# q, k and the attention scores laid out over four row groups, with a new order of the steps

## The chip, the cores and the metric

The kernel runs on one core of one Trainium2 chip. The metric is the device time of one execution in microseconds (us), from the first to the last instruction of the core; a profiled execution also gives the span and, for every engine, the instructions with their start and duration. The engines are called TensorE (PE in the profile, PEld for its weight loads), VectorE (DVE), ScalarE (ACT), GpSimd (POOL) and SyncE (SP, which issues the transfers). They run side by side[...], and semaphores tie them together.

## What is computed

Two layers of a "metaformer" over 32 images of 56 x 56 positions with 96 channels. Layer 0 is window attention (windows of 7 x 7 = 49 positions, three heads of 32 channels) and a feed-forward block, layer 1 a scan along the image's width (a linear recurrence, computed here as a product with a Toeplitz matrix) and a second feed-forward block. Cut to what the change touches:

```python
qkv = xs @ w_qkv + b_qkv                                   # 96 -> 3 x 96
q, k, v = (to_windows(t) for t in split(qkv))              # [image, head, window, 49, 32]
att = einsum('bhwid,bhwjd->bhwij', q, k) * scale + pos_bias
att = att.at[:, :, -nw_w:].add(ul_mask)
out = einsum('bhwij,bhwjd->bhwid', softmax(att), v)
x = x + (out @ w_out + b_out)
x = x + ffn0(norm(x));  x = x + scan(norm(x));  x = x + ffn1(norm(x))
```

## The kernel before

The work is cut into blocks: a quarter of an image, two rows of windows, 16 windows, 784 positions; 128 blocks in all. Everything that is done to a block is a *step* with a short name (`step[...]`, defined with `@steps`): `LD` loads it, `sa`, `pa`, `na`, `ta`, `ea` normalise and transpose it, `q`, `k`, `v` multiply by the weights on TensorE, `eq`, `ek`, `ev` copy the results out of PSUM on ScalarE, `sc` makes the scores, `st0` to `st2` scale them and add the bias on VectorE (one head each), `ex0` to `ex2` take the exponential on ScalarE, `av` multiplies by v, `rc` divides, `tro`, `eo`, `pr`, `ad` project and add. The feed-forward blocks are `s p n t e h x r c y z b k` with the letter `f` or `g`; `h` is a product on TensorE, `x` its copy to 16 bits on ScalarE, `r` bias and maximum on VectorE, `c` the cast to 8 bits (number 1 of three on GpSimd), `y` the second product, `k` the addition to the block on GpSimd. The scan has `se` to `xe`, `r0`, `pu0` to `pu3`, `th`, `uc`; six units `SC0` to `SC5` with `GA0` to `GA5` once per image, that is in every fourth block; then `gt`, `eg`, `so`, `as`. `ST` stores the block.

The order is written out by hand in a table (`PIPELINED`, line 55): a list of entries `name:lag`. The loop in `pipeline` (line 864) runs 140 iterations; iteration t issues, in the order of the table, every step for block t minus its lag. An extra dependency keeps each engine to exactly this order, so the table is the order of every queue. An iteration thus holds one step of each kind, of up to twelve different blocks; four iterations make an image, and one or two of the four hold the six scan units as well.

PSUM has four buffers of two banks (`banks`, line 117). Every step on TensorE takes one (`sc` two) and the reader's last instruction frees it; a step that finds none free waits. A second table, `IN_TURN`, and the steps `any` and `av_any` are for inputs outside a bound and do not run here.

`q` and `k` (line 515) are each two products: stationary 96 columns of the weights, moving 392 positions. A product in 32 bits appears in the trace as two weight loads and two matmuls, so each step has 4. The results lie in `qT` and `kT`, channels on partitions 0 to 95, a head on 32 of them, all 784 positions along the row. `scores` (line 554) takes each of 16 windows and 3 heads: stationary 64 keys of 32 channels, moving 49 queries. The three heads sit on three of the four groups of 32 rows of the array, even and odd windows on its two halves of 64 columns. The results of heads 0 and 1 fill the two banks of one buffer, those of head 2 one bank of a second.

Of the kernel before, what the change touches and what calls it, by code (L numbers as in the profile page):

```python
# [8 lines left out]
F32 = mybir.dt.float32  # L9
# [4 lines left out]
ALU = mybir.AluOpType  # L14
# [9 lines left out]
C = 96  # L24
# [3 lines left out]
NH = 3  # L28
HD = 32
# [8 lines left out]
NBLK = 4  # L38
NRP = NBLK * G
NTOK = G * TP  # L40
NPAIR = 8
W2 = WS * WS
OVER = 64 - W2
HALF = NPAIR * W2
MASKED = -1.0e30
LNC_EPS = 1e-6
LNT_EPS = 1e-5
SSM_EPS = 1e-3
QSCALE = float(C) ** -0.5
# [3 lines left out]


PIPELINED = (
    "pu0:4 SC5:8 bg:10 xf0:3 pu2:4 xf2:3 pu3:4 pg:9 ng:9 th0:4 sa:1 uc0:4 GA5:8 ex2:2 ex0:2 th2:4 "
    "rf2:3 hf1:3 rf0:3 pu1:4 uc2:4 tg:9 th3:4 uc3:4 xf1:3 uc1:4 av:2 pa:1 gt1:8 cf2:3 cf0:3 rf1:3 "
    "kg:10 rc:2 th1:4 SC3:7 eg:9 hg1:9 eg1:8 cf1:3 na:1 yf:3 xg1:9 zf:3 GA3:7 tro:2 bf:3 eo:2 hg2:9 "
    "kf:3 xg2:9 rg1:9 rg2:9 SC1:7 gt0:8 GA1:7 cg2:9 ST:11 hg0:9 eg0:8 pr:2 xg0:9 LD:0 ad:2 ta:1 ea:1 "
    "sf:2 se:3 SC4:7 pf:2 so:8 GA4:7 as:8 q:1 pe:3 nf:2 eq:1 v:1 cg1:9 ne:3 ev:1 SC2:7 rg0:9 k:1 "  # L60
    "cg0:9 ek:1 tf:2 sg:8 ef:2 SC0:7 GA2:7 GA0:7 te:3 sc:1 xe:3 st1:1 r0:3 st2:1 st0:1 yg:9 ex1:1 "
    "zg:9 hf0:2 hf2:2 "
)

IN_TURN = (
# [10 lines left out]
def kernel(  # L76
# [27 lines left out]
    nc = tc.nc  # L104
# [12 lines left out]
    def banks(name):  # L117

        return psum.tile([128, 2, 512], F32, tag="ps", name=name)
# [112 lines left out]
    n = 1  # L232
# [166 lines left out]
        vs.append(v)  # L399
    ot = const.tile([128, G, 2 * NPAIR, WS], F32, name="ot")  # L400
    nc.vector.memset(ot[C:], 1.0)
    qT = const.tile([C, NTOK + OVER], F32, name="qT")
    nc.vector.memset(qT[:, NTOK:], 0.0)
    kT = const.tile([C, NTOK + OVER], F32, name="kT")
    nc.vector.memset(kT[:, NTOK:], 0.0)
    pT = const.tile([128, NH, HALF + OVER], F32, name="pT")
    nc.vector.memset(pT[:, :, HALF:], 1.0)
    xs = const.tile([128, G, 3, RS], F32, name="xs")
# [84 lines left out]
    @steps("LD")  # L493
    def _(i):
        xb = xpool.tile([TP, G, C], F32, tag="xb", name=f"xb_{i}")
        for dst, src in block_dmas(i, x, xb):
            nc.sync.dma_start(dst, src)
        xtiles[i] = xb
# [15 lines left out]

    @steps("q", "k")
    def _(i, n):
        pq = banks(f"qk_{i}_{n}")
        for half in range(2):
            nc.tensor.matmul(  # L519
                pq[0:C, half, 0:HALF],  # L520
                wqkv[:, n * C : (n + 1) * C],
                xws[i % 2][:, half * HALF : (half + 1) * HALF],
                start=True,
                stop=True,
            )
        held["qk", i, n] = pq

    @steps("eq", "ek")
    def _(i, n):
        dst = (qT, kT)[n][:, 0:NTOK].rearrange("c (h t) -> c h t", h=2)  # L530
        nc.scalar.copy(dst, held.pop(("qk", i, n))[0:C, :, 0:HALF])  # L531

    @steps("v")
    def _(i):
# [17 lines left out]
        )  # L552

    def scores(i, stat, mov):
        pab, pc = banks(f"sab_{i}"), banks(f"sc_{i}")
        dst = [pab[:, 0], pab[:, 1], pc[:, 0]]
        for w in range(2 * NPAIR):
            p0, n0 = (w % 2) * 64, (w // 2) * W2
            for h in range(NH):
                hp = slice(h * HD, (h + 1) * HD)  # L560
                nc.tensor.matmul(
                    dst[h][p0 : p0 + 64, n0 : n0 + W2],
                    stat[hp, w * W2 : w * W2 + 64],
                    mov[hp, w * W2 : (w + 1) * W2],
                    start=True,
                    stop=True,
                )
        return [d[:, 0:HALF] for d in dst]

    def scaled(dst, i, ps):  # L570
        bt = bias[i % NBLK == NBLK - 1].rearrange("p w q -> p (w q)")
        nc.vector.scalar_tensor_tensor(dst, ps, QSCALE, bt, op0=ALU.mult, op1=ALU.add)  # L572


    @steps("sc")
    def _(i):
        held["s", i] = scores(i, kT, qT)

    @steps("st0", "st1", "st2")
    def _(i, h):  # L580
        scaled(pT[:, h, 0:HALF], i, held["s", i][h])

    @steps("ex0", "ex1", "ex2")
    def _(i, h):
# [2 lines left out]
    @steps("any")  # L587
    def _(i):

        for h, ps in enumerate(scores(i, qT, kT)):  # L590
            pr = one.tile([128, 8 * C], F32, tag="an", name=f"pr_{i}_{h}")
            nc.vector.memset(pr[:, HALF : HALF + OVER], 0.0)
            pa = pr[:, 0:HALF]
            p3 = pa.rearrange("p (w k) -> p w k", k=W2)
            scaled(pa, i, ps)
            mx = two.tile([128, NPAIR], F32, tag="mx", name=f"mx_{i}_{h}")
            nc.vector.tensor_reduce(mx, p3, op=ALU.max, axis=AX.X)
            nc.vector.tensor_tensor(p3, p3, mx[:, :, None].to_broadcast([128, NPAIR, W2]), ALU.subtract)
            nc.scalar.activation(pa, pa, AF.Exp)

            pp = banks(f"pp_{i}_{h}")
            for w in range(2 * NPAIR):
                p0, n0 = (w % 2) * 64, (w // 2) * W2
                nc.tensor.matmul(
                    pp[p0 : p0 + 64, 0, n0 : n0 + W2], pr[:, n0 : n0 + 64], ident[:, p0 : p0 + W2], start=True, stop=True
                )
            nc.scalar.copy(pT[:, h, 0:HALF], pp[:, 0, 0:HALF])
# [334 lines left out]
```

## Time and profile before

| What | Value |
|---|---|
| Median of 7 runs (lowest to highest) | 3890.18 us (3889.07 to 3901.09) |
| The profiled execution: its own time, and its span | 3903.86 us, 3902.1 us |
| ACT, POOL: share of the span | 61%, 37% |
| Row of `eq`: ACT L531, 96 x 784, mean | 808 ns |
| Row of `ek`: ACT L531, 96 x 784, mean | 811 ns |
| Row of `eo`: ACT L660, 96 x 392, mean | 515 ns |
| Row of `st0` to `st2`: DVE L572, 128 x 392, mean | 557 to 559 ns |

A share of busy time is an average over the whole span. A matmul's duration contains time in which the next one already runs, so for TensorE it is of more use to take the time from a step's start to the start of the next, which the timeline of the engine gives.

### The profile page before, as it was taken

The page shows a single profiled execution, that of the slowest core. Times are in us where ns is not written, and L with a number is a line of the kernel's source. Part 1 is how long each engine was busy: PE and PEld are TensorE (multiplying, and loading weights), DVE is VectorE, ACT ScalarE, POOL GpSimd, SP SyncE. Part 2 cuts the span into 40 slices and gives each one's busy share as a digit, 9 for nine tenths or more (in the row PEclk, how much of TensorE's full clock was granted, in tenths as well). Part 3 has the DMA queues.
Part 4 walks back from the last instruction along what each step waited for, and adds up shares of the span by engine and source line. Part 5 has one row for each costly group of instructions (what it writes and reads, how often), then busy time and mean ns, then how long its engine had stood idle before and what let it go on. Part 6 is the DMA issues. An engine that isn't in the chain of part 4 may idle for free.

```text
span 3902.1 us, 174541 instructions
## 1 busy us (share of the span) xinstructions
PE 3716.9 (95%) x76580; PEld 3174.4 (81%) x76580; DVE 3207.5 (82%) x9292; ACT 2392.9 (61%) x4611; POOL 1456.7 (37%) x1176
## 2 busy tenths in 40 slices
PE   2799999999999999999999999999999999999996
PEld 1688888888888888888888888888888888888874
DVE  3668888888888888888888888888888888888864
ACT  0656666666666666666666666666656666666652
POOL 1223334433334333334433333433333443333332
PEclk7989999999999999999999999999999999999996
DMA  6000111001101011001010010100100101001000
GB/s 129 17 3 22 25 24 26 23 22 25 25 22 28 21 24 25 22 22 28 23 26 21 22 28 21 28 21 22 27 23 22 27 21 28 21 22 28 18 15 21
DMA packets 226255, 99.12 MB, mean 25 GB/s; under 512 B 218396, under 2 KB 225150, under 8 KB 225262
## 3 DMA queue, kind: packets, MB, share of 16 engines
q1 hardware_dynamic: 222522, 86.81, 9.8%
q8 instruction: 606, 9.93, 1.0%
q10 hardware_dynamic: 2964, 1.05, 0.1%
q14 instruction: 163, 1.34, 0.1%
HBM read 44.45 MB, written 43.35 MB: 23 GB/s over the span
## 4 chain that ended last, share of the span: by engine, by line
PE 76%; DVE 17%; issue 2%; ACT 2%; DMA 2%; SPq 0%; POOL 0%; DVEq 0%; ACTq 0%; POOLq 0%
PE pu L778 12%; PE scan L802 10%; PE qk L519 6%; PE so L856 6%; PE av L622 5%; PE gt L835 5%; PE pu L779 4%; PE py_f L724 4%; PE ph_f L690 3%; PE pv L538 3%; PE tr_o L651 3%; DVE xn_f L457 3%; PE pr L670 3%; PE py_g L724 3%; PE ph_g L690 3%
## 5 line engine op out<-in xcount | busy, mean ns | idle before, releaser
L778 PE MATMUL pu<-weg,xs 128*128 128x288 f32 x1792 | 614.8, 425 | 9.2 <-ACT h_f L702 7.1
L802 PE MATMUL scan<-u,toep 64*64 64x28 f32 x24576 | 411.8, 221 | 19.5 <-issue 19.3
L802 PEld LDWEIGHTS scan<-u,toep 64*64 64x64 f32 x24576 | 386.7, 136 | 52.9 <-issue 42.9
L447 POOL TENSOR_TENSOR rs_a<-rs_a,neg_half 112x7 f32<-112x7 f32 x128 | 231.5, 1808 | 524.5 <-DVE rs_a L441 524.5
L779 PEld LDWEIGHTS pu<-weg,xs 128*128 128x128 f32 x1792 | 341.3, 190 | 95.5 <-issue 0.5
L519 PE MATMUL qk<-xw,wqkv 128*96 128x392 f32 x1024 | 393.7, 507 | 7.3 <-ACT xw L513 7.3
L746 POOL TENSOR_TENSOR xb<-xb,y_f 112x672 f32<-112x672 f32 x128 | 201.2, 1572 | 534.0 <-DVE y_f L742 398.2
L531 ACT COPY qT<-qk 96x784 f32<-96x784 f32 x128 | 103.5, 808 | 465.5 <-PE qk L519 465.5
L856 PE MATMUL so<-wso,gT 128*112 128x96 f32 x3584 | 374.9, 262 | 3.4 <-ACT gT L845 3.4
L856 PEld LDWEIGHTS so<-wso,gT 128*112 128x112 f32 x3584 | 362.3, 178 | 7.6 <-ACT gT L845 5.7
L447 POOL TENSOR_TENSOR rs_f<-rs_f,neg_half 112x7 f32<-112x7 f32 x128 | 190.6, 1489 | 462.9 <-DVE rs_f L441 462.9
L702 ACT CAST h_g<-ph_g 128x784 f16<-128x784 f32 x384 | 314.6, 821 | 69.2 <-PE ph_g L690 69.2
L767 POOL COPY xs<-xs 96x392 f32<-96x392 f32 x128 | 65.3, 510 | 759.7 <-issue 755.9
L845 ACT COPY gT<-gt 96x672 f32<-96x672 f32 (+1 forms) x256 | 209.3, 818 | 195.1 <-PE gt L835 195.1
L778 PEld LDWEIGHTS pu<-weg,xs 128*128 128x128 f32 x1792 | 280.4, 192 | 58.4 <-DVE pT L572 38.1
L779 PE MATMUL pu<-weg,xs 128*128 128x96 f32 x1792 | 321.2, 261 | 0.0
L702 ACT CAST h_f<-ph_f 128x784 f16<-128x784 f32 x384 | 307.0, 840 | 0.4 <-PE ph_f L690 0.2
L708 DVE TENSOR_SCALAR h_f<-h_f,b1q 128x784 f16<-128x784 f16 x384 | 276.0, 747 | 34.3 <-ACT h_f L702 33.8
L708 DVE TENSOR_SCALAR h_g<-h_g,b1q 128x784 f16<-128x784 f16 x384 | 208.4, 543 | 108.2 <-ACT h_g L702 108.2
L817 DVE SCALAR_TENSOR_TENSOR gt<-gt,scan 128x448 f32<-128x448 f32 x384 | 220.2, 615 | 78.8 <-PE scan L802 78.6
L457 DVE TENSOR_SCALAR xn_f<-xb,st_f,rs_f 112x96 fp8e5<-112x96 f32 x896 | 278.3, 385 | 3.0 <-POOL rs_f L447 3.0
L791 ACT COPY u<-pu 128x384 f32<-128x384 f32 (+1 forms) x512 | 228.3, 446 | 81.0 <-PE scan L802 45.5
(151 smaller groups left out, 9176.9 us busy)
## 6 DMA issues: line engine op xcount, KB each, us to landing
xb<-in_x_dram SPq DMA_DIRECT2D x224, 126.0 KB
out_dram<-xb SPq DMA_DIRECT2D x224, 126.0 KB
taps_d<-u SPq DMA_DIRECT2D x1, 4704.0 KB
xb<-in_x_dram SPq DMA_DIRECT2D x224, 13.1 KB
xb<-in_x_dram SPq DMA_DIRECT2D x224, 7.9 KB
out_dram<-xb SPq DMA_DIRECT2D x224, 13.1 KB
out_dram<-xb SPq DMA_DIRECT2D x224, 7.9 KB
xb<-in_x_dram SPq DMA_DIRECT2D x32, 72.0 KB
```

The source lines that it names most:

```text
L447: nc.gpsimd.tensor_tensor(rs, rs, neg_half, ALU.pow)
L457: nc.vector.tensor_scalar(xn[:, g, :], xb[:, g, :], mean[:, col], rs[:, col], op0=ALU.subtract, op1=ALU.mult, **saturate)
L519: nc.tensor.matmul(pq[0:C, half, 0:HALF], wqkv[:, n * C : (n + 1) * C], xws[i % 2][:, half * HALF : (half + 1) * HALF], start=True, stop=True,
L690: nc.tensor.matmul(ph[:, half, 0:HALF], w1q[:, hc * 128 : (hc + 1) * 128], xqs[layer][:, half * HALF : (half + 1) * HALF], start=True, sto ...
L702: nc.scalar.copy(h16.rearrange("p (h t) -> p h t", h=2), held.pop(("ph", n, i, hc))[:, :, 0:HALF])
L708: nc.vector.tensor_scalar(h16, h16, b1q[:, hc : hc + 1], 0.0, op0=ALU.add, op1=ALU.max)
L724: nc.tensor.matmul(po[:, g - g0, :], hq[hc][:, g * TP : (g + 1) * TP], w2q[:, hc, :], start=(hc == 0), stop=(hc == 2),)
L778: nc.tensor.matmul(pu[:, g, 0 : E + EH], rows[:, 0:128], weg[:, 0 : E + EH], start=True, stop=True)
L779: nc.tensor.matmul(pu[:, g, E + EH : 2 * E], rows[:, RS:], weg[:, E + EH :], start=True, stop=True)
L791: nc.scalar.copy(u[:, rp : rp + n, :], held["pu", i, j][:, 0:n, E : 2 * E])
L802: nc.tensor.matmul(py[o0 : o0 + RS, eh, e * NRP : (e + 1) * NRP], toep[p * RS : (p + 1) * RS, ch * HW : ch * HW + RS], u[p * RS : (p + 1) ...
L856: nc.tensor.matmul(po[:, g - g0, :], gT[:, g - g0, eh, :], wso[:, eh, :], start=(eh == 0), stop=(eh == 1))
```

## The change

It has two parts.

First, the layout. `qT` and `kT` give way to two arrays. `qk01` holds q and k of heads 0 and 1: its 128 partitions are four groups of 32, group g being head g mod 2 of the block's half g // 2 (eight windows). `qk2` holds q and k of head 2: group g is windows 4g to 4g + 3. The step named `q` now makes all of `qk01`, in four products (64 columns of weights, 392 positions), of which those of the two halves go to different halves of the array's columns. The step named `k` makes all of `qk2`, in eight products (32 columns of weights, 196 positions), the four quarters on the four column groups. `ek` copies 128 x 392 where it copied 96 x 784. `scores` has the same 48 products as before, but on all four row groups, each with a bank of its own in the same two buffers. Heads 0 and 1 are now each spread over both banks of one buffer, and head 2 over both buffers, so `st2` becomes two VectorE instructions of 128 x 196 and `st0`, `st1` read two runs of 196.

Second, the table `PIPELINED`. It has the same 117 steps in another order, most with a lag one higher; the store's lag is 11 as before, the load's 0. The scan units stood one behind `pu0`, then five in the next part of one iteration (`SC5:8`, and `SC3 SC1 SC4 SC2 SC0` with lag 7); now they are `SC1 SC3 SC4 SC2` in one iteration (lag 8) and `SC0 SC5` at the start of the next (lag 9).

```diff
 PIPELINED = (
-    "pu0:4 SC5:8 bg:10 xf0:3 pu2:4 xf2:3 pu3:4 pg:9 ng:9 th0:4 sa:1 uc0:4 GA5:8 ex2:2 ex0:2 th2:4 "
-    "rf2:3 hf1:3 rf0:3 pu1:4 uc2:4 tg:9 th3:4 uc3:4 xf1:3 uc1:4 av:2 pa:1 gt1:8 cf2:3 cf0:3 rf1:3 "
-    "kg:10 rc:2 th1:4 SC3:7 eg:9 hg1:9 eg1:8 cf1:3 na:1 yf:3 xg1:9 zf:3 GA3:7 tro:2 bf:3 eo:2 hg2:9 "
-    "kf:3 xg2:9 rg1:9 rg2:9 SC1:7 gt0:8 GA1:7 cg2:9 ST:11 hg0:9 eg0:8 pr:2 xg0:9 LD:0 ad:2 ta:1 ea:1 "
-    "sf:2 se:3 SC4:7 pf:2 so:8 GA4:7 as:8 q:1 pe:3 nf:2 eq:1 v:1 cg1:9 ne:3 ev:1 SC2:7 rg0:9 k:1 "
-    "cg0:9 ek:1 tf:2 sg:8 ef:2 SC0:7 GA2:7 GA0:7 te:3 sc:1 xe:3 st1:1 r0:3 st2:1 st0:1 yg:9 ex1:1 "
-    "zg:9 hf0:2 hf2:2 "
+    "rf2:4 r0:5 hf0:4 GA2:9 cf1:4 SC0:9 zg:11 GA0:9 ex2:3 ex0:3 pu1:5 SC5:9 xf0:4 pu0:5 th1:5 av:3 "
+    "cf2:4 GA5:9 bg:11 uc1:5 pu2:5 th0:5 sa:1 rc:3 ta:2 rf0:4 uc0:5 uc2:5 th2:5 cf0:4 pa:1 ea:2 pg:10 "
+    "tro:3 yf:4 eo:3 kg:11 gt0:9 zf:4 pr:3 ng:10 pu3:5 bf:4 eg0:9 kf:4 ad:3 th3:5 sf:3 uc3:5 pf:3 k:2 "
+    "tg:10 se:4 ek:2 pe:4 SC1:8 gt1:9 eg:10 eg1:9 q:2 GA1:8 eq:2 hg0:10 nf:3 xg0:10 hg1:10 rg0:10 "
+    "SC3:8 xg1:10 ne:4 so:9 SC4:8 as:9 hg2:10 GA3:8 ST:11 v:2 tf:3 cg0:10 GA4:8 xg2:10 sc:2 ev:2 te:4 "
+    "ef:3 rg1:10 hf1:3 xe:4 rg2:10 cg2:10 cg1:10 st1:2 st2:2 xf1:3 ex1:2 hf2:3 xf2:3 SC2:8 st0:2 "
+    "yg:10 sg:9 na:1 LD:0 rf1:3 "
 )
...
     @steps("q", "k")
     def _(i, n):
+        parts, h0, h1 = ((2, 0, 2), (4, 2, 3))[n]
+        size, rows = NTOK // parts, 128 // parts
         pq = banks(f"qk_{i}_{n}")
...
+        for m in range(2):
+            for j in range(parts):
+                nc.tensor.matmul(
+                    pq[j * rows : (j + 1) * rows, m, 0:size],
+                    wqkv[:, m * C + h0 * HD : m * C + h1 * HD],
+                    xws[i % 2][:, j * size : (j + 1) * size],
+                    start=True,
+                    stop=True,
+                )
+        held["qk", i, n] = pq[:, :, 0:size]
...
     @steps("eq", "ek")
     def _(i, n):
+        dst = (qk01[:, :, 0:HALF], qk2[:, :, 0:QUARTER])[n]
+        nc.scalar.copy(dst, held.pop(("qk", i, n)))
...
     def scores(i, stat, mov):
+        tiles = [banks(f"s{n}_{i}") for n in range(2)]
+
+        def product(src, size, g, w, col):
+            gp = slice(g * HD, (g + 1) * HD)
+            p0, n0 = (w % 2) * 64, col + w // 2 * W2
+            nc.tensor.matmul(
+                tiles[g % 2][p0 : p0 + 64, g // 2, n0 : n0 + W2],
+                src[gp, stat, w * W2 : w * W2 + 64],
+                src[gp, mov, w * W2 : (w + 1) * W2],
+                start=True,
+                stop=True,
+            )
+
+        for w in range(NPAIR):
+            for g in range(4):
+                product(qk01, HALF, g, w, 0)
+            if w % 2:
+                for w2 in (w // 2 * 2 % 4, w // 2 * 2 % 4 + 1):
+                    for g in range(2 * (w // 4), 2 * (w // 4) + 2):
+                        product(qk2, QUARTER, g, w2, QUARTER)
+        return tiles
```

## The prediction

> **What bounds the kernel now.** I read the page, then the groups by shape, the timeline of TensorE over one iteration, the stretches of one iteration and one image, and last the instruction queue in the DMA view.
>
> ```profile
> PE 3716.9 (95%) x76580; PEld 3174.4 (81%) x76580; DVE 3207.5 (82%) x9292; ACT 2392.9 (61%) x4611; POOL 1456.7 (37%) x1176
> ...
> PE 76%; DVE 17%; issue 2%; ACT 2%; DMA 2%; SPq 0%; POOL 0%; DVEq 0%; ACTq 0%; POOLq 0%
> ```
>
> TensorE is busy 95% and carries 76% of the chain of waits; VectorE carries most of the rest. Groups by shape:
>
> ```profile
> L802 PE MATMUL scan<-u,toep 64*64 64x28 f32 x24576 | 411.8, 221 | 19.5 <-issue 19.3
> L519 PE MATMUL qk<-xw,wqkv 128*96 128x392 f32 x1024 | 393.7, 507 | 7.3 <-ACT xw L513 7.3
> L538 PE MATMUL pv<-wqkv,xw 128*64 128x96 f32 x4096 | 199.7, 251 | 0.0
> L561 PE MATMUL sc<-qT,kT 32*64 32x49 f32 x4096 | 167.3, 224 | 3.5 <-issue 3.5
> ```
>
> The mean durations overlap, so I take starts from TensorE's timeline:
>
> ```profile
> 2023.55 1.48 PE L519 MATMUL qk<-xw,wqkv 128*96 128x392 f32 x4
> 2024.97 1.54 PE L538 MATMUL pv<-wqkv,xw 128*64 128x96 f32 x32
> 2026.44 1.56 PE L519 MATMUL qk<-xw,wqkv 128*96 128x392 f32 x4
> 2027.83 0.51 PE L470 MATMUL tr_f<-ident,xn_f 112*96 112x112 fp8e5 x7
> ```
>
> Start to start, q takes 1.42 us, v 1.47, k 1.39. Stretches (columns: length, then busy time of PE, PEld, DVE, ACT, POOL, granted clock, DMA):
>
> ```profile
> 2038.06:2063.40 25.34, 25.34 (x409) 21.54 (x407) 23.50 (x70) 18.45 (x37) 11.10 (x10) 1.00 0.11 26
> 2063.40:2104.46 41.06, 39.60 (x1176) 34.90 (x1174) 29.55 (x82) 19.00 (x37) 13.04 (x10) 0.96 0.08 19
> 2400.00:2515.40 115.40, 114.49 (x2395) 98.08 (x2394) 99.57 (x290) 74.46 (x145) 45.34 (x36) 1.00 0.10 24
> ```
>
> A plain iteration takes 25.34 us, an image 115.40. With every step of TensorE at the shortest interval it shows, a plain iteration is 25.0 and a scan unit 2.00, so an image would be 4 x 25.0 + 6 x 2.00 = 112.0. The other 3.4 us are waits: some 1.2 behind the scores (hf2 and pu0 wait for buffers that st2 and st0 free, 0.35 per iteration) and 2.2 around the scan units, the interesting ones:
>
> ```profile
> 2065.72 1.95 PE L802 MATMUL scan<-u,toep 64*64 64x28 f32 x118
> 2068.73 0.36 PE L802 MATMUL scan<-u,toep 64*64 64x28 f32 x10 [1.06 <-issue]
> 2069.02 0.61 PE L690 MATMUL ph_g<-xq,w1q 128*128 128x392 fp8e5 x2
> 2069.42 2.15 PE L724 MATMUL py_f<-w2q,hq_f 128*112 128x96 fp8e5 x21
> ```
>
> TensorE stands still with nothing to wait for: its instructions haven't arrived. Its instruction queue brings 606 packets, 9.93 MB, for 153160 instructions: about 256 each. In the busiest parts packets follow each other at no less than about 3.3 us, so some 76 instructions per us is the supply; a scan unit uses 256 in 2.00 us. The table sets where that bites: SC3 right behind av, sc right behind SC0.
>
> **What the Trainium skill says.** "TensorE: Matmul & The Clock Gate", Part 3, says small products in different row or column groups run at once. The trace agrees: pv, on two column halves, starts its matmuls in pairs 82 ns apart, so 32 take 1.47 us rather than 2.6. "TensorEngine Tiling (Array Packing)", Tiling Modes, says that changing the tiling mode drains the engine. The trace shows a price: tr_e before the scores takes 0.76 us where tr_a, the same shape before a full product, takes 0.67; tr_g before av 0.44, tr_f 0.35; pv's end adds about 0.09 again. "TensorE: Matmul & The Clock Gate", Part 1, halves the clock after idling; after the stop above the clock was 0.50 from 2070 to 2072. "SBUF — State Buffer", Who interferes with whom, says that GpSimd and VectorE's fast modes lock one pair of ports against each other. Timelines of VectorE, then GpSimd:
>
> ```profile
> 2037.62 1.70 DVE L708 TENSOR_SCALAR h_f<-h_f,b1q 128x784 f16<-128x784 f16 x1
> ```
> ```profile
> 2037.64 1.46 POOL L746 TENSOR_TENSOR xb<-xb,y_g 112x672 f32<-112x672 f32 x1
> ```
>
> That step takes 0.42 us elsewhere in the same iteration.
>
> **The change, part by part.**
>
> *q and k.* A pass over 392 positions takes 0.33 us (1.32 for four), and each product is two passes. New q: 4 products, 8 passes on two column halves, 4 x 0.33 = 1.32, no less than before. New k: 16 passes of 196 positions on four groups, 4 x 0.166 = 0.66. Ends cost as v's: 1.47 - 16 x 0.082 = 0.15 each, and entering the mode 0.09. Before, q stood next to v and v next to k, so three steps shared two changes; the new order is gt1 q hg0, pu3 k tg, hg2 v tf, so each pays its own: q 1.32 + 0.24 = 1.56, k 0.66 + 0.24 = 0.90, v 1.56, sum 4.02 against 4.27. Gain 0.25 per block. Bounds: four column groups are not shown. If only two run at once k is 1.57 and the step loses 0.4; if the mode changes cost nothing it gains 0.65.
>
> *Scores.* Now 96 passes lie on six tiles of the array, 16 each, from first to last start 1.04 us: 65 ns per pass; SC needs 58 on four tiles. On eight tiles 12 passes x 0.062 + 0.15 = 0.89; but head 2 loads groups 0 and 1 in the first half and 2 and 3 in the second, and if the queue can't reach across it is 16 x 0.062 + 0.15 = 1.14. I take 1.02 against 1.19: 0.17 per block, bounds 0.05 and 0.3.
>
> *The other engines.* st2 becomes two instructions; from the rows of L489 (384 elements 553 ns, 288 448) half of 392 saves 0.21 of the 0.475 us from start to start, so two take 0.52: 0.05 more on VectorE. ek falls from 811 to about 515 ns (row of eo, same length); ScalarE, 18.45 busy in 25.34, gains nothing on the path.
>
> *Supply.* k and q have 32 more instructions per block (+4%). What counts is the instructions in a stretch against 76 per us, plus the 64 that the engine's queue holds by the first table of the page on TensorE (no run here shows that number). Before: SC2, k, tf, SC0, te, sc have 740 in 7.8 us (593 supplied, 80 short); av, gt1, SC3 have 460 in 4.3 us (327, 70 short). New, the worst runs from SC4 through v, sc, SC2, SC0, SC5 to av: 1590 in 19.2 us (1460, 66 short); no single unit stands next to av or sc without 0.7 us of long products between. One shortage in place of two, and it comes after SC1 and SC3 with room around them: of the 2.2 us I leave 0.9 + 0.2 for mode changes. Gain 1.1 per image; bounds 2.0 and -0.8 (several stops, each with a half clock).
>
> *Transfers.* SP holds only ST and LD. ST waits for kg, LD for ST; kg moves up to lag 11, so a load comes about one iteration nearer to its use. The load then lies between kg (about 10 us into an iteration) and sa of the next one, some 20 us, against about 5 us for a store and a load seen in the DMA view. No cost.
>
> *Waits of the new order.* After sc come te, hf1, hf2, yg. te and hf1 take 1.09 us; st1 and st2 need 1.0 and a handover, st0 0.5 more: hf2 and yg together wait about 0.35, as before. ScalarE's chain ev, ef, xe, xf1, ex1, xf2 ends 1.6 us into the next iteration, before pu0 needs xf2's buffer, and ex0 ends just as av wants it (3.2 us). So I charge the same 1.2 per image.
>
> *Both ends.* In both tables the second load stands behind the large Toeplitz transfer (sa waits 41.1 us for it once), and from sa at lag 1 to ST at lag 11 there are as many iterations. Nothing.
>
> Sum: 128 x (0.25 + 0.17) = 54, 32 x 1.1 = 35, together 89 us. Profiled execution 3903.86 - 89 = 3815, times 3890.18 / 3903.86 (the profiled run lies 0.35% above the median): **3802 us**.
>
> **Rivals.**
>
> *The array gives nothing* (four column groups in pairs, or mode changes eat it): only the supply's 35, less some for k: about 3856. For it: nothing before shows four groups; against: pv's pairs.
>
> *The order also removes VectorE's waits*, and the supply stops fully: 54 + 38 + 64 = 156, 3735. For it: 3.4 us per image are there to take. Against: VectorE is busy 23.5 of 25.34.
>
> *Slower: VectorE's loop decides.* Place: from the end of pr, VectorE must do ad 0.85, sf 1.2, wait for pf on GpSimd 0.35 beyond se 1.2, nf 2.25, rg0 0.42, ne 1.7, as 0.85, cg0 0.5, rg1, rg2 0.84, cg2 0.5, st1, st2 1.0: 11.7; then TensorE from hf2 through yg to the end of the next pr: 12.5; handovers 0.2. The loop is 24.4 us, with TensorE's own 24.9 just above. rf2 now comes with cf1 on GpSimd, rg2 with cg1, each able to block it 0.8 us or more. With one on the loop it is 25.2, as before; with two 26.0. Beyond 1.0 us of blocking the change loses: with 1.9 in every iteration, an image is 4 x 26.3 + 12.0 + 0.9 = 118.1, +2.7: 3976. In half the iterations it is about no change.
>
> **How the numbers follow.** Forecast 0.50 (its own range 3765 to 3845), array gives nothing 0.16, waits gone too 0.09, slower 0.25, of which 0.05 ends near no change; 0.03 of the second does as well. Below 0.2% nothing can be told apart here (the runs before mostly lie within that). So faster 0.72, same 0.08, slower 0.20. The range takes in both ends of the bounds, 3735, and on the other side the milder half of the loop's cases: 3915.
>
> **What would show it.** Right: k from start to start near 0.8 us plus a mode change, q still 1.4 to 1.5, scores near 1.0; plain iterations of 24.6 to 25.1; TensorE's waits for "issue" in the scan below 30 us in all. Wrong: k at 1.4 or more; stops of 1 us with the clock at 0.5 in many images; hf2, yg or yf waiting for VectorE by more than 0.7 us per iteration, with a 16-bit step of 1.2 us or more ahead of it.

## The result, and the profile after

The changed kernel takes 3879.58 us (median of 15 runs, 3874.93 to 3888.66), beside 3891.55 us for the kernel before on the same chip (35 runs). The ratio is 0.9969, with a 95% interval of 0.9963 to 0.9976. So it is faster by 0.3%, which is outside the noise, and by 12 us where 88 us were forecast; 3802 us lies far off, and the range (3735 to 3915) holds the time. The profiled execution took 3876.86 us, its span is 3875.1 (before: 3902.1). The profiled execution of the kernel before was a long one, 12 us above the median of its kernel, so the two pages lie 27 us apart where the kernels lie 12 apart.

Two lines of the page of the changed kernel, the busy time of the engines and the shares of the chain of waits:

```profile
PE 3699.8 (95%) x78628; PEld 3126.1 (81%) x78628; DVE 3244.9 (84%) x9420; ACT 2330.7 (60%) x4611; POOL 1453.5 (38%) x1176
...
PE 90%; DVE 6%; DMA 2%; issue 1%; ACT 0%; POOL 0%; SPq 0%; ACTq 0%; DVEq 0%; POOLq 0%
```

TensorE's share of the chain went from 76% to 90%, VectorE's from 17% to 6%. By itself that says little: the page of the new layout with the old table, a slower kernel, has 88% and 3%. TensorE is still busy 95%, so "busy" says nothing of the change either. Its groups by shape:

```profile
L830 PE MATMUL scan<-u,toep 64*64 64x28 f32 x24576 | 408.3, 221 | 15.3 <-issue 14.2 <-ACT u L819 0.5
L526 PE MATMUL qk<-xw,wqkv 128*64 128x392 f32 x1024 | 198.6, 509 | 0.3 <-issue 0.3
L545 PE MATMUL pv<-wqkv,xw 128*64 128x96 f32 x4096 | 197.6, 249 | 0.0
L568 PE MATMUL s<-qk 32*64 32x49 f32 x12288 | 172.0, 228 | 1.7 <-issue 1.7
L526 PE MATMUL qk<-xw,wqkv 128*32 128x196 f32 x2048 | 112.8, 338 | 2.3 <-ACT xw L516 2.3
```

q and k together are busy 311 us where they were 394, the scores 172 where they were 170 (both groups of line 561 together). TensorE's timeline in one plain iteration (start, duration; the distance to the next start is what counts), k first and then the scores with what follows them:

```profile
1912.41 0.87 PE L526 MATMUL qk<-xw,wqkv 128*32 128x196 f32 x16
1913.21 0.54 PE L473 MATMUL tr_g<-ident,xn_g 112*96 112x112 fp8e5 x7
...
1921.60 1.31 PE L568 MATMUL s<-qk 32*64 32x49 f32 x96
1922.85 0.88 PE L475 MATMUL tr_e<-ident,xn_e 112*96 112x112 f32 x7
1923.56 0.50 PE L718 MATMUL ph_f<-xq,w1q 128*128 128x392 fp8e5 x2
1924.24 0.51 PE L718 MATMUL ph_f<-xq,w1q 128*128 128x392 fp8e5 x2 [0.18 <-DVE pT L599]
1924.71 1.24 PE L752 MATMUL py_g<-w2q,hq_g 128*112 128x96 fp8e5 x21
```

k takes 0.80 us from start to start (1.39 before), so all four column groups do work side by side. The scores take 1.25 (1.20 before). And hf1 (1923.56) is followed by hf2 only 0.68 us later, where the product needs 0.34: hf2 waits for VectorE's reading of the scores. VectorE's timeline has that reading, four instructions that take 1.70 us together and begin 0.26 us after the start of the last product:

```profile
1922.95 1.70 DVE L599 SCALAR_TENSOR_TENSOR pT<-s,bias 128x392 f32<-128x392 f32 x4 [0.25 <-PE s L568]
```

The stretch of this iteration (length, busy time of PE, PEld, DVE, ACT, POOL, clock, DMA):

```profile
1903.72:1929.01 25.29, 25.11 (x423) 21.14 (x422) 23.49 (x71) 17.91 (x38) 11.23 (x9) 1.00 0.11 26
```

25.29 us, beside 25.34 before: 0.05 us of the 0.25 + 0.17 per block that q and k and the scores were to bring.

### The profile page after: what moved, and what is told of

Read it like the earlier page. It is cut to its first block, busy times and chain, and to the rows that moved or that the text cites. A ratio compares the mean times of both kernels' runs of the same rounds, so it can differ in the third digit from the quotient of the medians.

```text
span 3875.1 us, 178068 instructions
## 1 busy us (share of the span) xinstructions
PE 3699.8 (95%) x78628; PEld 3126.1 (81%) x78628; DVE 3244.9 (84%) x9420; ACT 2330.7 (60%) x4611; POOL 1453.5 (38%) x1176
## 3 DMA queue, kind: packets, MB, share of 16 engines
q14 instruction: 161, 1.32, 0.1%
## 4 chain that ended last, share of the span: by engine, by line
PE 90%; DVE 6%; DMA 2%; issue 1%; ACT 0%; POOL 0%; SPq 0%; ACTq 0%; DVEq 0%; POOLq 0%
PE pu L806 13%; PE scan L830 10%; PE so L884 9%; PE qk L526 7%; PE av L650 5%; PE gt L863 5%; PE pv L545 5%; PE pr L698 5%; PE pu L807 5%; PE s L568 4%; DVE pT L599 4%; PE py_g L752 4%; PE ph_g L718 4%; PE py_f L752 4%; PE tr_o L679 3%; PE ph_f L718 3%
## 5 line engine op out<-in xcount | busy, mean ns | idle before, releaser
L730 ACT CAST h_g<-ph_g 128x784 f16<-128x784 f32 x384 | 300.4, 821 | 346.6 <-issue 329.1
L460 DVE TENSOR_SCALAR xn_g<-xb,st_g,rs_g 112x96 fp8e5<-112x96 f32 x896 | 366.9, 477 | 91.8 <-POOL rs_g L450 91.5
L830 PE MATMUL scan<-u,toep 64*64 64x28 f32 x24576 | 408.3, 221 | 15.3 <-issue 14.2
L742 POOL CAST hq_g<-h_g 128x784 fp8e5<-128x784 f16 x128 | 123.0, 961 | 751.1 <-DVE h_g L736 472.8
L450 POOL TENSOR_TENSOR rs_a<-rs_a,neg_half 112x7 f32<-112x7 f32 x128 | 190.8, 1491 | 548.2 <-DVE rs_a L444 548.2
L814 ACT ACTIVATE gt<-pu 128x384 f32<-128x384 f32 (+1 forms) x512 | 238.1, 465 | 205.9 <-PE pu L807 205.9
L526 PE MATMUL qk<-xw,wqkv 128*32 128x196 f32 (+1 forms) x3072 | 311.0, 395 | 2.7 <-ACT xw L516 2.3
L650 PE MATMUL av<-v,pT 64*64 64x33 f32 x12288 | 212.1, 223 | 59.6 <-ACT pT L612 59.1
L718 PEld LDWEIGHTS <-w1q 128*128 128x128 fp8e5 x1536 | 122.5, 100 | 172.5 <-issue 78.4
L650 PEld LDWEIGHTS av<-v,pT 64*64 64x64 f32 x12288 | 197.0, 137 | 72.7 <-ACT pT L612 59.8
L599 DVE SCALAR_TENSOR_TENSOR pT<-s,bias 128x392 f32<-128x392 f32 (+1 forms) x512 | 213.6, 459 | 49.9 <-PE s L568 45.5
```

Of the source, the lines that this page charges most:

```text
L460: nc.vector.tensor_scalar(xn[:, g, :], xb[:, g, :], mean[:, col], rs[:, col], op0=ALU.subtract, op1=ALU.mult, **saturate)
L526: nc.tensor.matmul(pq[j * rows : (j + 1) * rows, m, 0:size], wqkv[:, m * C + h0 * HD : m * C + h1 * HD], xws[i % 2][:, j * size : (j + 1) ...
L599: nc.vector.scalar_tensor_tensor(view(dst), src, QSCALE, view(bt), op0=ALU.mult, op1=ALU.add)
L650: nc.tensor.matmul(po[r * 64 : r * 64 + 64, k, n0 : n0 + HD + 1], pT[kp, h, pair * W2 : pair * W2 + 64], v[kp, pair * NH + h, :], start=Tr ...
L718: nc.tensor.matmul(ph[:, half, 0:HALF], w1q[:, hc * 128 : (hc + 1) * 128], xqs[layer][:, half * HALF : (half + 1) * HALF], start=True, sto ...
L730: nc.scalar.copy(h16.rearrange("p (h t) -> p h t", h=2), held.pop(("ph", n, i, hc))[:, :, 0:HALF])
```

## The experiments

All ratios are to the kernel before on the same chip, with 95% intervals; the changed kernel's is 0.997. The runs were made on several chips (the kernel before had medians from 3891 to 3912 us on them), so times of different chips aren't compared. "A step's interval" is the mean time from its start to the start of the next step on TensorE, over the 24 middle images; "plain iteration" is one without scan units, counted from one av or k to the next, and its length is the median. An "iteration with scan units" is counted so that all six lie in one. A scan unit's "stop" is what its interval exceeds 2.00 us by.

Stops have to be compared on one chip. Summed over a whole run they were 42 to 69 us in the seven profiles of one chip, 32 to 35 in three of a second, 23 to 29 in four of a third; the kernels differ within each group, but the groups don't overlap.

### One part alone

The new table on the old layout:

```diff
 PIPELINED = (
-    "pu0:4 SC5:8 bg:10 ...
+    "rf2:4 r0:5 hf0:4 GA2:9 ...
...
```

> The layout of before (q and k over 96 channels, scores on three row groups) in the new order. If TensorE's own time sets the pace, the k step goes back from 0.80 to 1.39 us and only some 0.2 us of mode changes and of q are saved per block: +0.4 us x 128 = about +50 us on the changed kernel, 3930 us. If VectorE's loop through the scores swallows what TensorE gains, the time stays within 15 us of the changed kernel's 3880.

Measured: 0.9965 (0.9952 to 0.9978). The table alone gives all of the measured gain. Its plain iteration is 25.17 us, shorter than the changed kernel's.

The new layout with the old table (the two lines of the diff above the other way round, everything else of the change kept):

> The new layout in the order of before, where q, v and k stand next to each other. If TensorE's own time sets the pace: k 0.59 us shorter, q up to 0.1 longer, scores no shorter: about -0.45 us x 128 = -58 us on the kernel before, 3833 us. If VectorE (23.5 us busy of 25.34 in a plain iteration) sets it: 3880 to 3892, no gain.

Measured: 1.014 (1.011 to 1.0169). The layout alone makes the kernel slower. TensorE's and then VectorE's timeline of one of its plain iterations (25.71 us long):

```profile
1940.44 1.36 PE L475 MATMUL tr_e<-ident,xn_e 112*96 112x112 f32 x7
1941.73 1.31 PE L568 MATMUL s<-qk 32*64 32x49 f32 x96
...
1944.09 0.50 PE L718 MATMUL ph_f<-xq,w1q 128*128 128x392 fp8e5 x2
1944.92 0.51 PE L718 MATMUL ph_f<-xq,w1q 128*128 128x392 fp8e5 x2 [0.33 <-DVE pT L599]
```

```profile
1937.42 2.35 DVE L460 TENSOR_SCALAR xn_f<-xb,st_f,rs_f 112x96 fp8e5<-112x96 f32 x7
1939.69 1.75 DVE L460 TENSOR_SCALAR xn_e<-xb,st_e,rs_e 112x96 f32<-112x96 f32 x7
...
1943.65 1.69 DVE L599 SCALAR_TENSOR_TENSOR pT<-s,bias 128x392 f32<-128x392 f32 x4
```

The old order was bound by VectorE. TensorE reaches tr_e earlier thanks to the short k, and then goes at the pace of xn_e: tr_e takes 1.29 us up to the scores' start, 0.76 in a plain iteration of the kernel before. Most of what k saves (0.59 us) is lost there at once. On VectorE the four readings take 1.69 us, three took 1.50; they lie on the loop that decides, and the plain iteration goes from 25.34 to 25.71. So the longer reading accounts for about half of these 0.37 us; the rest was not taken apart.

### What the scores are limited by

Head 2's products by turns to groups 0, 1 and 2, 3, so that all groups are loaded evenly:

```diff
-                for w2 in (w // 2 * 2 % 4, w // 2 * 2 % 4 + 1):
-                    for g in range(2 * (w // 4), 2 * (w // 4) + 2):
+                for w2 in (w // 4 * 2, w // 4 * 2 + 1):
+                    for g in range(w // 2 % 2 * 2, w // 2 % 2 * 2 + 2):
```

> The changed kernel with the products of head 2 spread evenly: behind each pair of windows they go by turns to row groups 0 and 1 or 2 and 3, not the first half of them all to 0 and 1. If the uneven load is why the scores did not get shorter, they fall from 1.25 to about 1.0 us: -0.2 us x 128 = -25 us or more, 3850. If the number of products per step or the supply of instructions is the limit, the step stays at 1.2 to 1.25 us and the time at 3880.

Measured: 0.9987 (0.9965 to 1.0008), the scores' shortest interval is 1.24 us as in the changed kernel. The uneven load is not the limit.

Half of the products left out, the rest twice as wide:

```diff
-                tiles[g % 2][p0 : p0 + 64, g // 2, n0 : n0 + W2],
+                tiles[g % 2][p0 : p0 + 64, g // 2, n0 : n0 + 2 * W2],
...
-                src[gp, mov, w * W2 : (w + 1) * W2],
+                src[gp, mov, w * W2 : (w + 2) * W2],
...
-        for w in range(NPAIR):
+        for w in (0, 1, 4, 5):
```

> The changed kernel with half of the score products left out and the other half 98 queries wide in place of 49: the same columns stream through the array, in 48 passes in place of 96. Theory 'a score pass costs its start, about 11 ns per weight load and matmul, however many groups of the array it finds free': sc goes from 1.24 us to about 0.7. Rival 'the columns that stream decide': sc stays at 1.2 to 1.3. Either way 96 instructions per block less are to be supplied; if supply cost what I had charged (1.1 us per image), the scan's stops shrink by some 0.5 to 1 us per image. Ratio about 0.985 under the first, 0.993 to 0.997 under the second.

Measured: 0.9854 (0.9833 to 0.9876). TensorE's timeline:

```profile
1899.68 0.99 PE L568 MATMUL s<-qk 32*64 32x98 f32 x48
1900.60 0.88 PE L475 MATMUL tr_e<-ident,xn_e 112*96 112x112 f32 x7
```

The scores take 0.92 us: neither theory's number. From the first to the last start, 96 passes of 49 columns need 1.10 us (11.6 ns each), 48 of 98 need 0.75 (15.9 ns). If a pass costs a fixed part and a part per column, that is about 7.3 ns and 4.3 ns per 49 columns (an estimate from these two points). The larger part goes with the pass: six tiles took 1.06 us for the same 96 passes, eight take 1.10. The order of the passes counts a little: in the run below with heads 0 and 1 first, the 96 take 1.00 us at the shortest.

The run shows a second thing. The scores shrink by 0.35 us per block, 45 us in all, and the kernel gains the same (0.9969 to 0.9854 is 45 us). With the new table, what TensorE saves is paid in full. So nothing off TensorE took the layout's gain; it should be found on TensorE's own path.

### The wait behind the scores

yg placed ahead of hf1, to fill TensorE's time while VectorE reads the scores:

```diff
-... ef:3 rg1:10 hf1:3 xe:4 rg2:10 cg2:10 cg1:10 st1:2 ... st0:2 yg:10 sg:9 ...
+... ef:3 rg1:10 rg2:10 cg2:10 cg1:10 yg:10 hf1:3 xe:4 st1:2 ... st0:2 sg:9 ...
```

> The changed kernel with yg put between te and hf1 (rg2, cg2, cg1 listed ahead of it; no other queue's order changes). If TensorE waits 0.47 us per block only because st1, st2 and st0 take longer than te and hf1, the wait is covered by yg: -0.4 us x 128 = about -50 us, 3830 us. If VectorE's loop sets the pace it has only the 0.25 us per iteration that it waits for the scores to give: at most -30 us, more like 3860.

Measured: 1.0073 (1.0047 to 1.01). The wait at hf2 is gone and stands at pu1 instead, by TensorE's timeline:

```profile
1963.89 0.75 PE L806 MATMUL pu<-weg,xs 128*128 128x288 f32 x2 [0.28 <-ACT h_f L730]
```

By the order of the table, yg, hf1, hf2 and hf0 hold all four PSUM buffers, and pu1 has to wait until ScalarE's xf1 has emptied one. The plain iteration is 25.36 (25.29 in the changed kernel); the larger loss lies in the scan units, whose stops sum to 67 us here and to 42 in the run with even scores on the same chip. Why they grew, this run doesn't explain.

st2's two halves in the other order, so that the buffer of st1 comes free first:

```diff
-                for n in range(2)
+                for n in (1, 0)
```

> The changed kernel, with the two VectorE instructions of st2 in the other order: the half in the buffer that st1 reads comes first, so that this buffer is free after st1 and one half of st2, 0.26 us earlier than in the changed kernel; nothing is left out. Theory 'the doubled st2 eats what the layout gains': hf1 to hf2 falls from 0.68 us to about 0.45, the plain iteration from 25.3 to about 25.1, ratio against the kernel before about 0.991 to 0.993 (the changed kernel: 0.997). Rival 'VectorE's loop decides the iteration': hf1's 0.2 us come back as a wait elsewhere (pu1, yf or tr), ratio 0.996 to 0.998.

Measured: 0.9976 (0.9967 to 0.9986). TensorE's timeline shows where hf2's wait went:

```profile
1922.20 0.83 PE L718 MATMUL ph_f<-xq,w1q 128*128 128x392 fp8e5 x4
1923.35 1.24 PE L752 MATMUL py_g<-w2q,hq_g 128*112 128x96 fp8e5 x21 [0.32 <-DVE pT L599]
```

hf1 and hf2 go together now, and yg waits, for the end of st0 and the second buffer. The first buffer was never the point: TensorE has te, hf1 and hf2 to do and is through with them 1.54 us after the last product's start; then it needs the second buffer, which is free only 1.96 us after that start (0.26 until the reading begins, 1.70 for the reading).

Heads 0 and 1 first in the scores, st1, st0, st2 in this order, to begin the reading earlier:

```diff
         for w in range(NPAIR):
             for g in range(4):
                 product(qk01, HALF, g, w, 0)
-            if w % 2:
...
+        for w in range(NPAIR // 2):
+            for g in range(4):
+                product(qk2, QUARTER, g, w, QUARTER)
```

> The changed kernel, with all products of heads 0 and 1 ahead of those of head 2 (which then use all four row groups by turns), and st1, st0, st2 in this order. st1 can start before the last products have ended, and both score buffers are free after st1, st0, st2. Theory 'the steps behind the scores wait for the reading of the scores by VectorE, 1.7 us long, and nothing else': st1 starts where the cast cg2 ends, about 0.25 us earlier, hf2 and yg wait that much less, the plain iteration falls from 25.3 to about 25.1, ratio 0.990 to 0.993 (changed kernel: 0.997). Rival 'the wait goes on to the next step' (yg, pu1 or av waits instead, as in the two reorderings before): 0.996 to 0.998.

Measured: 1.0116 (1.0083 to 1.0149). And the same with rg2, cg2 ahead of rg1, so that VectorE is free early:

> As the run with heads 0 and 1 first, and rg2, cg2 placed ahead of rg1, so that GpSimd's cast cg1 starts behind rg1 and VectorE's cast cg2 no longer runs beside it (1.08 us beside it, 0.56 alone). VectorE is then free some 0.5 us before the scores are ready and st1 starts as soon as the products of heads 0 and 1 are done, 0.5 to 0.6 us earlier than in the changed kernel. Theory of the reading: no wait is left at hf2 and yg, plain iteration about 24.95, ratio 0.985 to 0.988. Rival 'the wait goes on to the next step': 0.993 or more, with pu1 waiting for xf1, or av for ex0.

Measured: 1.0105 (1.0087 to 1.0123). VectorE's timeline of the latter:

```profile
1909.26 0.57 DVE L741 CAST hq_g<-h_g 128x784 fp8e5<-128x784 f16 x1
1910.98 1.70 DVE L598 SCALAR_TENSOR_TENSOR pT<-s,bias 128x392 f32<-128x392 f32 x4 [0.82 <-PE s L568]
```

The cast takes 0.57 as expected and VectorE stands waiting for 0.82 us, but st1 still begins only 0.28 to 0.29 us after the last of all products has started: it waits for the whole step, not for the part it reads. So the expectation's premise was wrong, and the edit couldn't test what it was to test. What it does show is that VectorE's lateness is not the wait's cause: half a microsecond more of slack changed nothing (plain iteration 25.31). What is lost lies in the iterations with scan units (41.8 and 40.9 us; 40.4 in the run with even scores on the same chip), where above all SC2 stops more (2.63 and 2.51 us, 2.10 there); why this order of products does that stayed open.

st2 in two instructions, on the old layout with the new table:

```diff
...
-        scaled(pT[:, h, 0:HALF], i, held["s", i][h])
+        for c in ((0, HALF),) if h < 2 else ((0, QUARTER), (QUARTER, HALF)):
+            scaled(pT[:, h, c[0] : c[1]], i, held["s", i][h][:, c[0] : c[1]], c)
```

> The kernel before with the new table, and its st2 cut into two VectorE instructions of 196 columns, as the new layout makes it; nothing else of the layout. Theory 'the second instruction of st2 costs its start on the path': hf1 to hf2, or hf2 to yg, longer by 0.15 to 0.25 us, iteration from 25.17 to 25.35 to 25.4, ratio 1.001 to 1.005 (the new table alone: 0.9965). Rival 'the wait in the changed kernel comes from the scores' start or from somewhere else': 0.996 to 0.998.

Measured: 0.9995 (0.9982 to 1.0007), between what the two theories expect. The plain iteration grows by 0.07 us, hf1's interval from 0.47 to 0.54. The reading, first start to last end, goes from 1.51 to 1.57 us; in the changed kernel it is 1.70. Two neighbouring halves cost only 0.06 more than one instruction. The other 0.13 comes with the new layout's halves, which lie between each other in the rows of pT: the first of them takes 0.39 us to the next start, in whichever order they stand, and 0.27 here. Why was not taken apart.

Last, each of the two score buffers read whole, in one instruction. pT and the bias get the layout of the scores, and av takes its operands from there:

```diff
+WIDE = QUARTER + QUARTER // 2
...
-    pT = const.tile([128, NH, HALF + OVER], F32, name="pT")
+    pT = const.tile([128, 2, 2, WIDE + OVER], F32, name="pT")
...
-    @steps("st0", "st1", "st2")
+    @steps("st0", "st1")
+    def _(i, n):
+        bt = bias[i % NBLK == NBLK - 1].rearrange("p b w q -> p b (w q)")
+        nc.vector.scalar_tensor_tensor(
+            pT[:, n, :, 0:WIDE], held["s", i][n][:, :, 0:WIDE], QSCALE, bt, op0=ALU.mult, op1=ALU.add
+        )
...
-                            pT[kp, h, pair * W2 : pair * W2 + 64],
+                            pT[kp, n, b, o0 : o0 + 64],
```

> The changed kernel, with pT and the bias laid out like the scores, so that VectorE reads each of the two score buffers whole, in one instruction of 588 elements (st1, then st0; st2 and ex2 are gone, their work is in the two others). Four instructions that take 1.70 us from the first start to the last end become two, 1.45 to 1.55 us, and the first buffer is free after the first of them, 0.4 us earlier than now; ScalarE issues two exponentials in place of three. Theory 'what the layout saves on q and k is given back in the reading of the scores, which hf2 and yg wait for': hf2's wait is nearly gone, yg starts 2.85 to 2.95 us after the scores' start (now 3.14), plain iteration 25.0 to 25.15, ratio 0.989 to 0.993. Rival 'VectorE's or ScalarE's loop stands right behind': plain iteration stays at 25.25 or more, ratio 0.995 to 0.998, with the wait now at pu1 or av.

Measured: 0.9911 (0.9897 to 0.9925), the fastest kernel here that computes everything. TensorE's timeline, VectorE's, and the stretch of a plain iteration:

```profile
1912.98 1.31 PE L569 MATMUL s<-qk 32*64 32x49 f32 x96
1914.22 0.88 PE L476 MATMUL tr_e<-ident,xn_e 112*96 112x112 f32 x7
1914.94 0.83 PE L735 MATMUL ph_f<-xq,w1q 128*128 128x392 fp8e5 x4
1915.83 1.24 PE L769 MATMUL py_g<-w2q,hq_g 128*112 128x96 fp8e5 x21
```

```profile
1914.33 1.45 DVE L616 SCALAR_TENSOR_TENSOR pT<-s,bias 128x588 f32<-128x588 f32 x2 [0.25 <-PE s L569]
```

```profile
1895.10:1920.14 25.04, 24.98 (x424) 21.17 (x423) 23.28 (x69) 17.83 (x36) 11.23 (x9) 1.00 0.12 27
```

The reading takes 1.45 us, hf1 and hf2 go together, yg starts 2.85 us after the scores (3.11 in the changed kernel), and the iteration is 25.04. With the reading shortened by 0.25 us the plain iteration gains 0.25 us. The whole kernel gains less, some 23 us and not 32: its scan units stop for 43 us in this run, and the changed kernel wasn't run on that chip.

Set beside the new table on the old layout, this shows where the layout's gain had gone. TensorE's timeline there:

```profile
1913.02 1.48 PE L519 MATMUL qk<-xw,wqkv 128*96 128x392 f32 x4
1914.34 0.51 PE L470 MATMUL tr_g<-ident,xn_g 112*96 112x112 fp8e5 x7
...
1924.36 1.01 PE L690 MATMUL ph_f<-xq,w1q 128*128 128x392 fp8e5 x4
1925.35 1.24 PE L724 MATMUL py_g<-w2q,hq_g 128*112 128x96 fp8e5 x21
```

The medians of the intervals in plain iterations, in us (all other steps agree within 0.004):

| Steps | New table, old layout | Changed kernel | Two readings |
|---|---|---|---|
| k | 1.32 | 0.80 | 0.80 |
| q | 1.32 | 1.47 | 1.47 |
| pu3, tg, gt1, hg0 beside them | 2.05 | 2.28 | 2.28 |
| sc | 1.20 | 1.25 | 1.25 |
| hf1 and hf2 | 0.94 | 1.15 | 0.90 |
| the iteration | 25.17 | 25.29 | 25.04 |

On the same table the layout saves 0.52 us in k, but q and the neighbours of both pay 0.38 more for changes of mode that the old layout didn't need there: 0.13 are left. The scores take 0.04 of it, and the longer reading costs 0.21 at hf1. So the layout alone turns a gain of 0.13 into a loss of 0.12, and with the shorter reading the gain is there.

### VectorE's wait, and what it covers

In the changed kernel VectorE waits 0.9 us per iteration for pg on GpSimd, behind pa. pa moved behind pg in the table:

```diff
-... cf0:4 pa:1 ea:2 pg:10 tro:3 ...
+... cf0:4 ea:2 pg:10 pa:1 tro:3 ...
```

> The changed kernel, with pa placed behind pg in the table, so that GpSimd does pg first. VectorE's wait for rs_g (0.9 us in each plain iteration of the changed kernel) goes, and xn_g (2.9 us beside kg) starts earlier. Theory 'TensorE and the latency behind the scores decide, VectorE is fed early enough': TensorE's steps keep their intervals, ratio 0.996 to 0.998. Rival 'VectorE's loop decides': up to 0.9 us less per iteration, ratio 0.96 to 0.99.

Measured: 1.0226 (1.0204 to 1.0247), slower than either theory allows. GpSimd's and VectorE's timelines, then TensorE's:

```profile
1955.30 1.50 POOL L450 TENSOR_TENSOR rs_a<-rs_a,neg_half 112x7 f32<-112x7 f32 x1 [0.43 <-DVE rs_a L444]
1956.75 1.46 POOL L774 TENSOR_TENSOR xb<-xb,y_g 112x672 f32<-112x672 f32 x1
```

```profile
1956.79 1.85 DVE L742 CAST hq_f<-h_f 128x784 fp8e5<-128x784 f16 x1
1958.56 1.75 DVE L460 TENSOR_SCALAR xn_g<-xb,st_g,rs_g 112x96 fp8e5<-112x96 f32 x7
```

```profile
1958.69 1.28 PE L752 MATMUL py_f<-w2q,hq_f 128*112 128x96 fp8e5 x21 [0.79 <-DVE hq_f L742]
```

The wait is gone, but with pg done early, GpSimd's addition kg comes 1.4 us earlier and falls on VectorE's cast. The cast then takes 1.85 us in place of 0.58, the product yf waits 0.79 us for it, and the plain iteration goes from 25.3 to 26.3. In the changed kernel the same addition fell on xn_g (2.90 us there, 1.75 here), which nobody on the path waits for. The Trainium skill ("SBUF — State Buffer", Who interferes with whom) says that GpSimd and VectorE's fast modes lock one pair of ports against each other. The trace agrees and shows the price for one cast, 1.27 us; only its place decides whether it costs anything.

Both edits, the swapped halves of st2 and pg ahead of pa:

> Both of the two edits before: st2's halves swapped, pg ahead of pa. If the wait behind the scores was latency alone, this is as the first edit alone (0.991 to 0.993); if VectorE's loop stood right behind it, the second edit lets the first one pay and only the two together gain (about 0.99, each alone 0.996 to 0.998).

Measured: 1.0226 (1.0205 to 1.0248), the same as the second alone, for the same reason.

### The ends of the run, or the supply of instructions

The kernel before, the changed kernel and the new table on the old layout, unchanged, profiled on one chip:

> The kernel before, unchanged, profiled on the same chip as the next two, because how often the scan units run out of instructions differs between runs. If the two ends of the run carry the gain of the new table: the ninth av starts near 303 us, the last quarter-images as long as in the first profile (352 us from av 120 to the end), and the 112 blocks between take as long as with the new table alone, within 8 us. If the supply of instructions carries it: the blocks between take 20 us or more longer than with the new table alone.

> The changed kernel, unchanged, on the same chip. Ends as in its first profile: ninth av near 289 us, 341 us from av 120 to the end, together some 25 us less than the kernel before; the 112 blocks between within 8 us of the kernel before. The scan units' stops about as long in sum as in the kernel before on this chip (within 10 us).

> The kernel before with the new table alone, on the same chip: ninth av near 290 us, ends together some 17 us less than the kernel before; plain iterations of 25.2, 0.1 shorter than those of the changed kernel; scan units' stops as in the changed kernel if they belong to the chip and the order (in the two profiles so far, on different chips, 48 and 27 us), larger by 20 us if they belong to the old layout.

Measured, 0.9993 (0.9978 to 1.0009), 0.9965 (0.9955 to 0.9975) and 0.9963 (0.9942 to 0.9983), and in the three profiles, in us:

| Part of the run | before | changed | new table alone |
|---|---|---|---|
| start, to the ninth av | 300.7 | 290.8 | 291.1 |
| 112 blocks, to av 120 | 3237.9 | 3243.6 | 3224.0 |
| from there to the last product | 352.3 | 342.7 | 348.4 |
| scan units over 2.00 us each, whole run | 34.3 | 31.8 | 34.7 |

In the changed kernel the ends carry the gain: 19.5 us, while its middle is 5.7 us *longer* than that of the kernel before. The table alone saves 13.5 at the ends and 13.9 in the middle, which fits neither of the two expectations (within 8 us, or 20 and more); the layout on top of it costs 19.6 in the middle and saves 6.0 at the ends. The scan units' stops for instructions stayed the same within 3 us.

Each column is one execution, and the two parts differ in how well they repeat. In the first profiles of the kernel before and of the changed kernel the ends sum to 654.6 and 629.2 us (653.0 and 633.5 here), in the first of the table alone to 637.2 (639.5 here). The middle of one and the same kernel moves more: 3231.2 and 3243.6 us for the changed kernel, 3245.4 and 3224.0 for the table alone. So the gain at the ends, 19 to 25 us, is clear in both pairs. Of the middle only the plain iterations are (25.34, 25.29 and 25.17 us in both profiles of each kernel); the sums of 112 blocks move with the stops.

What shortens the start is seen in TensorE's waits from 40 to 305 us (us in total, times, longest), before and then changed, and in the stretches:

```profile
PE tr_o L651 <- DVE an L641: 41.1, 4, 40.2
PE pu L778 <- ACT h_f L702: 7.1, 1, 7.1
PE pr L670 <- ACT ot L660: 5.4, 6, 1.1
PE qk L519 <- ACT xw L513: 5.0, 5, 1.0
```

```profile
PE av L650 <- ACT pT L612: 60.4, 3, 49.5
...
PE pr L698 <- ACT ot L688: 1.0, 1, 1.0
```

```profile
150.00:200.00 50.00, 43.60 (x703) 33.20 (x704) 34.95 (x119) 29.27 (x58) 17.69 (x14) 1.00 0.01 2
200.00:250.00 50.00, 47.88 (x1235) 40.47 (x1234) 26.91 (x78) 20.71 (x41) 9.33 (x8) 0.80 0.01 3
```

```profile
150.00:200.00 50.00, 49.61 (x805) 39.09 (x804) 36.79 (x116) 31.17 (x66) 18.13 (x15) 0.98 0.01 2
200.00:250.00 50.00, 47.53 (x1412) 40.27 (x1410) 35.24 (x99) 25.13 (x51) 11.94 (x11) 1.00 0.02 4
```

Both pay the long wait for the second load (most of 41.1 and of 60.4; in the new order it stands at another step). But while the pipeline fills, the old order leaves TensorE waiting for the copies of the same block (pr for ot, qk for xw), and an iteration takes 22.3 us where the new one takes 20.0. Up to the ninth av all of TensorE's waits sum to 68.3 us before and 67.5 changed: the wait for the load is 19 us longer in the new order, because TensorE stands there with less work behind it, and the other waits are 20 us shorter. That these make up the 9.9 us is argued from the two profiles; no run took them apart. The clock doesn't decide between them: the first scan units run at 0.80 before and at 1.00 in the new order, but from 100 to 150 us it is the other way round (0.90 and 0.77), and from 40 to 305 us the mean is 0.85 in both.

In the last part, from av 120 on, TensorE's waits sum to 40.0 us before, 28.5 in the changed kernel and 29.2 with the table alone; the largest is that of tr_g for xn_g (11.9, 7.9 and 9.5). What in the order shortens them was not tested.

## Why the prediction was right or wrong

The direction was right by luck: the terms that were to bring the gain sum to about nothing, and the one that was put at nothing brought all of it. The table below sets the terms beside what two pairs of profiles show, in us per image (24 middle images, sums of intervals; a minus is a gain).

| Term | Forecast | First profiles | One chip |
|---|---|---|---|
| q, k, v with their neighbours pu3, tg, gt1, hg0, hg2 | -1.0 | -1.4 | -1.4 |
| scores (shortest interval, and tf, te beside them) | -0.7 | +0.4 | +0.5 |
| waits behind the scores (hf0 to hf2, yg) | 0 | +0.8 | +0.8 |
| supply of instructions, and all the rest | -1.1 | -0.1 | +0.5 |
| together | -2.8 | -0.3 | +0.4 |
| both ends, per run | 0 | -25.4 | -19.5 |

So per image 2.5 to 3.2 us of the forecast didn't come: 1.1 to 1.2 of them in the scores, 0.8 in the waits behind them, 1.0 to 1.6 in the supply and the rest; q, k and v were 0.4 better.

**q and k: right.** k measured 0.80 plus 0.09 at pu3 ahead of it, against 0.90; q 1.48 plus 0.05 at gt1, against 1.56; v with hg2 1.54, against 1.56. Four column groups run side by side and each change of mode is paid for. But this gain belongs to layout and table together: the table alone already takes q and k to 1.32 us each, since neither stands next to v there, and on the same table the layout brings 0.13 us per block and not 0.25.

**Scores: the term failed.** I took a pass as 62 to 65 ns on its tile, so that eight tiles would need 12 passes' time. The measured cost goes mostly with the pass itself (about 7 of 11.6 ns), on six tiles or eight, and the even distribution changed nothing. The shortest interval went from 1.18 to 1.24 instead of to 1.02.

**"So I charge the same 1.2 per image": this step failed, and made a loss of the layout's gain.** (By the 0.35 per iteration that I read it should have been 1.4; it stood on both sides, so the sum is the same.) The forecast put st1 and st2 at 1.0 us, with st0 0.5 behind, and let hf2 and yg wait 0.35 together. Measured, the reading takes 1.70 and begins 0.26 behind the last product's start, so hf1's interval alone is 0.34 us too long. I had priced st2's second instruction on VectorE's busy time (0.05 us) and not on what waits for it. Shortening the reading by 0.25 brought 0.25 per iteration, and shortening the scores by 0.35 brought 0.35.

**Supply: the term failed.** 35 us were forecast; on one chip the scan units' stops fell from 34.3 to 31.8 us in the whole run, and within the scores 0.5 us per image were saved (sc's mean comes closer to its shortest), while pu0 to pu2 and av became 1.1 us longer per image (0.7 of it stops, the rest a longer shortest interval beside other neighbours). The stops moved from SC3, SC1 and sc to SC0, SC5 and the steps between. Counting instructions per stretch said where they could stand, not how often. Nor could the sign that I named decide it: "issue below 30 us" in the scan's row held before the change already (19.3 us, 14.2 after).

**Ends: "Nothing" was wrong.** I compared the lags and the second load, which are indeed alike, and not the order within an iteration, which decides how often TensorE waits when few blocks are in flight. The ends gave all of the measured gain; which waits in them did it is argued above and not shown.

Of the rivals, the slower one, VectorE's loop, is the case of the layout with the old table (1.014). What it says of blocking is seen with pg ahead of pa (1.0226): 1.27 us by GpSimd in every iteration, on a step that TensorE waits for, cost 1.0. In the changed kernel GpSimd's blocking was there as feared, on other steps than I named (xn_g at 2.90 in place of 1.75, two casts at 1.08 in place of 0.57), but on none that TensorE waited for.

## What to carry to other kernels

When a product's results move into other buffers, price the reading as well: count what its reader needs from the last product until each buffer is free, and compare that with the work that stands between the product and the next step that needs a buffer. A faster engine gives nothing while a wait of that kind follows it; shortening the wait (one instruction per buffer instead of four pieces) gave 0.25 us per iteration, the layout's products 0.13. Price a new layout against the old one on the same order, too, or what the order gives is counted for the layout. And judge an order by the filling and emptying of the pipeline too: here 19 to 25 us in two stretches of some 300 us outweighed everything in between.

## What the runs showed of the hardware that wasn't expected

A reading of 128x588 from two PSUM banks takes 0.69 us to the next start, less than twice the 0.39 of a 128x196 one whose other half lies between its rows; three of 392 take 1.51, two of 588 take 1.45. A 16-bit to 8-bit cast of 128x784 on VectorE takes 0.57 alone, 1.08 beside a cast on GpSimd and 1.85 beside a GpSimd addition of 112x672. And products of 32 rows by 64 columns with 49 moving columns follow each other at 11.1 ns on six tiles of the array and at 10.5 to 11.6 ns on eight, by their order: a third more tiles brought next to nothing.
